# Softmax denominators of two non-local blocks: from matmuls with ones on TensorE to 32x32 transposes on VectorE

## The chip, the cores and the metric

The kernel runs on one core of a Trainium2 chip. The metric is the device time of one execution in microseconds (us). All data are float32. Engines are named as in the profile: PE is TensorE (PEld its weight loads), DVE is VectorE, ACT is ScalarE, SP is SyncE, which here only issues transfers (DMAs).

## The reference, cut to what matters

The input x has 4 images of 128 channels and 96 x 96 pixels. Two non-local blocks with weights of their own follow each other; each is

```python
g_x = maxpool2(conv1x1(x, g_w, g_b)).reshape(b, CI, -1).transpose(0, 2, 1)
theta_x = conv1x1(x, theta_w, theta_b).reshape(b, CI, -1).transpose(0, 2, 1)
phi_x = maxpool2(conv1x1(x, phi_w, phi_b)).reshape(b, CI, -1)
f = jnp.einsum('bqc,bck->bqk', theta_x, phi_x)
attn = jax.nn.softmax(f, axis=-1)
y = jnp.einsum('bqk,bkc->bqc', attn, g_x)
...
W_y = conv1x1(y, W_w, W_b)
...
return W_y + x
```

with CI = 64 inner channels, 9216 queries (pixels) and 2304 keys (pooled pixels) for each image, and a batch normalisation of W_y that is folded into the weights. Each query's softmax has one denominator: the sum of 2304 exponentials. This change is about these sums, their inverses, and how the inverses get to where they are multiplied.

## The kernel before

**Tiles.** An image and a layer make a block; there are 8, in the order of ORDER. A block's 9216 queries are taken in 9 *pairs* of 1024, two halves of 512 queries each; 72 pairs in all. Keys come in 18 tiles of 128. For a key tile, `scores` puts exp(theta . phi - 35) of 128 keys by 1024 queries into an `exp` tile (four matmuls of 64x64 by 512 columns, one ACT operation), `add_up` adds the tile into the pair's `sum` (128 x 1024) on DVE, and `values` accumulates values times exponentials in PSUM (`av`, four matmuls). Every matmul of the program is two instructions in the trace. A constant shift of 35 takes the place of the row maximum; whether it was enough is checked at the end from notes of all denominators and inverses.

**Steps.** The loop over `t` makes a step out of two key tiles of one pair. A pair has 9 steps, and a *cycle* has 18, s = 0 to 17: the even pair of the cycle in steps 0 to 8, the odd one in 9 to 17. In step t PE does the scores of step t and then the values of step t - 1. The order on PE, DVE, ACT and SP is the order in which the program's text issues the instructions[...]. Into the steps other work is put by hand: `first` goes between the two scores of a step, `second` after them, ahead of the values; `take` between the step's two adds on DVE; the rest behind the values.

**A pair's end.** After its last values, ACT copies `av` to `halves` (128 x 1024), and DVE adds its two halves into y (128 x 512) in `add_halves`. The column sums of `sum` over 128 partitions are the denominators. Half of each pair's partitions lies in the wrong place for that, so `move` sends 64 partitions of `sum` (256 KB) by a DMA on SP's queue to the tile `folded`, and `fold` adds the other 64 on DVE (L422). In step 2 of the next cycle (SUMS), `denominators` multiplies `folded` with a matrix of ones (L494): this sums over partitions and puts each result on 64 partitions at once. ACT takes the result out of PSUM (L413) and notes its sum; DVE inverts it in four pieces of 128 columns (L409), one a step; ACT notes the sum of the inverses (L426); DVE multiplies y with them (`normalise`, L433).

**The projection.** `multiply` (L439) projects y by W into two banks of PSUM, and `add` (L448) adds the shift and x on DVE and, for the second layer, stores 1024 columns of x to memory. The even pair is normalised in step 6 and projected in step 8, the odd one in 10 and 12 (PROJECT).

**Shared banks.** Two banks of PSUM (`misc`) serve in turn the denominators, the thetas (step 5), the chunks of the next block's keys (three steps of a cycle: 13, 15 and 17, in three cycles of each block; each goes on into the step after it, where DVE pools its result), and the projections.

Of the kernel before, what the change touches and what calls it, by code (L numbers as in the profile page):

```python
# [32 lines left out]
PT = 2 * QT  # L33
NP = HW // PT
KB = 2
NB = NKT // KB
FIRST = 6
KEYS = (15, 17, 31)
THETAS, SUMS, PROJECT = 5, 2, (8, 12)
EXPS = 7  # L40
WARM = (5, 3)
CYCLE = 2 * NB
ORDER = ((0, 0), (1, 0), (0, 1), (2, 0), (1, 1), (3, 0), (2, 1), (3, 1))
# [3 lines left out]

@with_exitstack
def shifted_blocks(ctx: ExitStack, tc: tile.TileContext, x: bass.AP, layers, out: bass.AP, flag):

# [19 lines left out]
    nc = tc.nc  # L70

    const = ctx.enter_context(tc.tile_pool(name="const", bufs=1))
# [3 lines left out]
    work = ctx.enter_context(tc.tile_pool(name="work", bufs=2))  # L76
# [13 lines left out]
    nc.vector.memset(nshift, -SHIFT)  # L90
    ones = const.tile([P, CI], F32, name="ones")
    nc.vector.memset(ones, 1.0)
    dens = const.tile([P, len(ORDER) * NP + 1], F32, name="dens")
    recs = const.tile([P, len(ORDER) * NP + 1], F32, name="recs")
    for t in (dens, recs):
        nc.vector.memset(t, 0.0)

    def load_x(b, n=6):
        xt = xp.tile([C, HW], F32, tag="x", name=f"x_{b}")
# [90 lines left out]
    def two_banks(name):  # L190
        return [ps_misc.tile([P, QT], F32, tag="misc", name=f"{name}_{i}") for i in range(2)]
# [108 lines left out]
    class Pair:  # L300
# [74 lines left out]
        def last_denominators(self):  # L375

            n = QT // 2
            self.rc, notes = self.sum[:, :QT], []
            for i in range(2):
                den = ps_sc.tile([P, PT], F32, tag="sc", name=f"den_last_ps_{i}")[:, :n]  # L380
                for part in (self.sum, self.es[NKT - 1]):
                    for h in range(2):
                        nc.tensor.matmul(
                            den[ts(h, CI), :], lhsT=ones,
                            rhs=part[:, h * QT + i * n : h * QT + (i + 1) * n],
                            start=part is self.sum, stop=part is not self.sum,
                        )
                notes.append(den)
            for i in (0, 1):
                for k in range(n // P):  # L390
                    nc.vector.reciprocal(
                        self.rc[:, ts(i * n // P + k, P)], notes[i][:, ts(k, P)]
                    )
                if i == 0:
                    self.sum_up(notes[1], dens, 1)
            self.sum_up(notes[0], dens, 0)
            for i in range(2):
                self.sum_up(self.rc[:, ts(i, n)], recs, i)

        def sum_up(self, src, to, i):  # L400

            n = self.number + i
            nc.scalar.activation(
                self.th[:, : src.shape[1]], src, AF.Identity, accum_out=to[:, n : n + 1]
            )

        def inverses(self, src, pieces=range(QT // P)):
            for i in pieces:
                nc.vector.reciprocal(self.rc[:, ts(i, P)], src[:, ts(i, P)])  # L409

        def take_denominators(self, ps, to):
            n, self.rc = self.number, to
            nc.scalar.activation(to, ps, AF.Identity, accum_out=dens[:, n : n + 1])  # L413

        def move(self, folded):

            i = self.number % 2
            nc.sync.dma_start(out=folded[ts(i, CI), :], in_=self.sum[ts(1 - i, CI), :])

        def fold(self, folded):  # L420
            here = ts(self.number % 2, CI)
            nc.vector.tensor_add(folded[here, :], folded[here, :], self.sum[here, :])  # L422

        def note(self, to):
            n = self.number
            nc.scalar.activation(to, self.rc, AF.Identity, accum_out=recs[:, n : n + 1])  # L426

        def add_halves(self):
            self.y = self.halves[:, :QT]
# [25 lines left out]
        def finish(self, check, result):  # L455
# [20 lines left out]
            for i in range(2):  # L476
# [6 lines left out]
                    nc.sync.dma_start(out=self.blk.store[:, first : first + n], in_=dst)  # L483
                if i == 0:
                    result(good)

    def denominators(both, folded):

        pss = two_banks(f"den_ps_{both[0].name}")

        def make():
            for h in range(2):
                for i in range(len(both)):
                    nc.tensor.matmul(  # L494
                        pss[i][ts(h, CI), :], lhsT=ones[ts(i, CI), :],
                        rhs=folded[ts(i, CI), ts(h, QT)], start=True, stop=True,
                    )

        def take():
            for pair, ps in zip(both, pss):  # L500
                pair.take_denominators(ps, pair.halves[:, QT:])

        return make, take

    def thetas(both):
        pss = two_banks(f"theta_ps_{both[0].name}")
# [41 lines left out]
    pairs = [Pair(blk, p, n * NP + p) for n, blk in enumerate(blocks) for p in range(NP)]  # L548
    total = len(pairs) * NB
# [43 lines left out]
    for n in range(1, len(blocks)):  # L593
        cycle = (n - 1) * NP * NB // CYCLE * CYCLE
        for j in range(NB):
            t = cycle + KEYS[j % len(KEYS)] + j // len(KEYS) * CYCLE
# [2 lines left out]
                centres[t + 2] = blocks[n]  # L599
            if j % len(KEYS) == len(KEYS) - 1:  # L600
                spreads[t + 2] = (blocks[n], j // len(KEYS))
    loads = {4 * NB + 4: 2, 31 * NB + 4: 3}
    late = len(pairs) - 2

    ends = {
        total - 3: (NKT - 8,), total - 2: (NKT - 7,), total - 1: (NKT - 6, NKT - 5),
        total: range(NKT - 4, NKT),
    }
    folded, gone, pending = None, [], (None, None)
    for t in range(total + 1):  # L610
        q, s = 2 * (t // CYCLE), t % CYCLE
        even, odd = pairs[q : q + 2] if t < total else (None, None)
        first, second, take = None, *pending
        pending = (None, None)
        if t in keys:
            n, i = keys[t]
            if n and i == 0:
                begin(n)
            first, *pending = blocks[n].chunks(i)
        elif t < total and s == (THETAS if q else THETAS + 1):  # L620
            if q < late:
                first, *pending = thetas(pairs[q + 1 : q + 3])
            else:
                first, take = odd.theta_alone()
        elif gone and s == SUMS:
            second, take = denominators(gone, folded)
        elif q == late and s == 11:
            second, take = denominators([even], folded)
        elif t == total - 1:
            second, take = even.multiply, even.add  # L630
        elif gone and s in PROJECT:
            pair = gone[PROJECT.index(s)]
            second, take = pair.multiply, pair.add
        if t < total:
            now, j = divmod(t, NB)
            if s == 0 and q:
                pairs[q - 1].move(folded)
                gone = pairs[q - 2 : q]
            if s == NB:
                folded = work.tile([P, PT], F32, tag="folded", name=f"folded_{q}", bufs=1)  # L640
                even.move(folded)
            if t in loads:
                xs[loads[t]] = load_x(loads[t])
        for i in range(KB):
# [3 lines left out]
                first()  # L648
        if second:
            second()  # L650
        if gone and s == 1:
            gone[1].fold(folded)
        if q == late and s == 10:
            even.fold(folded)
        for i in range(KB):
            if t < total:
                pairs[now].add_up(j * KB + i)
# [1 line left out]
                take()  # L659
        if t - 1 in keys and t < NB:  # L660
            b0.batch(keys[t - 1][1])
        if t == total - 1:
            even.note(even.rc)
        if gone and s in (PROJECT[0] - 1, PROJECT[1] - 1):
            pair = gone[s // (PROJECT[1] - 1)]
            pair.note(pair.rc)
        if t:
            before, j = divmod(t - 1, NB)
            for k in ends.get(t, range(j * KB, (j + 1) * KB)):
                pairs[before].values(k)  # L670
        if t < total:
            for i, pair in enumerate(gone):
                if s == 1:
                    pair.add_halves()
                k = s - PROJECT[i] + 5
                if k in range(QT // P):
                    pair.inverses(pair.rc, (k,))
                if k == QT // P - 1:
                    pair.normalise()
            if s == 13 and q < late:  # L680
                even.fold(folded)
            if q == late:
                if s == 10:
                    even.add_halves()
                if s - 12 in range(QT // P):
                    even.inverses(even.rc, (s - 12,))
                if s == 15:
                    even.normalise()
        if t == total - 1:
            odd.last_denominators()  # L690
        if t in centres:
# [17 lines left out]
    def check():  # L709

        ps = ps_sc.tile([P, PT], F32, tag="sc", name="good_ps")[:1, :1]
        nc.vector.tensor_reduce(good[:, 0:1], dens, AX.X, ALU.add)
        nc.vector.tensor_scalar(good[:, 1:2], good[:, 0:1], SUM_MAX, None, ALU.is_le)
        nc.vector.tensor_reduce(good[:, 0:1], recs, AX.X, ALU.add)
# [314 lines left out]
```

## Time and profile before

| | |
|---|---|
| median of 3 runs | 2527.51 us (2527.16 to 2528.47) |
| the profiled execution | 2528.21 us |
| its span, first to last instruction | 2526.1 us |
| granted TensorE clock | 0.999 |
| DMA traffic | 60.12 MB, mean 24 GB/s |
| PE instructions | 23342 |

The span is what the views of the trace cover; 2.1 us of the profiled execution lie outside it. In a line of a group, the fields are: line of the program, engine, operation, output and inputs, shapes, count, busy us and mean ns of one, and the engine's idle time just before them with what ended it. In a list of waits: who waited for whom, us in total, times, the longest. In a timeline: start, us from the first start to the last end, what, how many; where a line merges several instructions, their number is behind the x. Line numbers here and in the groups are those of the kernel before.

### The profile page before, as it was taken

The numbers are of one execution on the slowest core, as the hardware profiler recorded it, in microseconds if no ns is written. First come the engines' busy times: TensorE is split into PE (matmuls) and PEld (weight loads), VectorE is DVE, ScalarE is ACT, GpSimd is POOL, SyncE is SP. The second block draws the span as 40 slices with busy tenths as digits, with TensorE's granted clock in tenths as the row PEclk, the third lists the DMA queues.
The fourth block names the chain that finished last, engine by engine and source line by source line (L and its number), as shares of the span: only waits on it lengthen the run. The fifth ranks groups of instructions, "written<-read, shape, count | busy, mean of one in ns | idle before, by whom it ended". The sixth has DMA issues, their size and how long they took to land.

```text
span 2526.1 us, 53450 instructions
## 1 busy us (share of the span) xinstructions
PE 2514.9 (100%) x23342; PEld 908.8 (36%) x23342; DVE 2167.2 (86%) x2259; ACT 1626.7 (64%) x1795; POOL 0.7 (0%) x6
## 2 busy tenths in 40 slices
PE   9999999999999999999999999999999999999998
PEld 4333333333333333333333333333333333333333
DVE  7888888888888888888888888888888888888888
ACT  5666666666666666666666666666666666666665
POOL 0000000000000000000000000000000000000000
PEclk9999999999999999999999999999999999999999
DMA  4020000000000000020000000000000000000001
GB/s 159 5 85 9 10 10 5 10 9 10 10 18 14 26 26 26 18 80 10 10 10 18 23 17 26 26 18 9 6 10 10 24 20 14 26 26 26 26 26 40
DMA packets 16661, 60.12 MB, mean 24 GB/s; under 512 B 2650, under 2 KB 3556, under 8 KB 16420
## 3 DMA queue, kind: packets, MB, share of 16 engines
q1 hardware_dynamic: 16252, 56.57, 7.4%
q8 instruction: 184, 3.01, 0.5%
q14 instruction: 57, 0.47, 0.1%
q10 hardware_dynamic: 168, 0.07, 0.0%
HBM read 19.14 MB, written 18.87 MB: 15 GB/s over the span
## 4 chain that ended last, share of the span: by engine, by line


## 5 line engine op out<-in xcount | busy, mean ns | idle before, releaser
L349 ACT ACTIVATE exp<-sc,nshift 128x1024 f32<-128x1024 f32 x1296 | 1386.1, 1113 | 814.5 <-PE sc L343 814.4
L358 DVE TENSOR_TENSOR sum<-sum,exp 128x1024 f32<-128x1024 f32 x1151 | 1408.2, 1223 | 258.0 <-ACT exp L349 207.7
L343 PE MATMUL sc<-theta,phi 64*64 64x512 f32 x10368 | 1251.0, 589 | 0.8 <-ACT exp L349 0.8
L366 PE MATMUL av<-exp,gT 64*64 64x512 f32 x10368 | 1232.3, 589 | 0.0
L366 PEld LDWEIGHTS av<-exp,gT 64*64 64x64 f32 x10368 | 399.8, 133 | 713.0 <-issue 689.6
L343 PEld LDWEIGHTS sc<-theta,phi 64*64 64x64 f32 x10368 | 399.2, 133 | 712.9 <-issue 649.1
L409 DVE RECIPROCAL halves<-halves 128x128 f32<-128x128 f32 x284 | 268.5, 945 | 0.0
L200 PE MATMUL gphi_ps<-x,gphiT 64*64 64x512 f32 x1056 | 137.3, 589 | 0.0
L356 DVE TENSOR_TENSOR sum<-exp,exp 128x1024 f32<-128x1024 f32 x72 | 88.1, 1224 | 49.2 <-ACT exp L349 48.5
L226 DVE TENSOR_REDUCE gphi<-gphi_ps 128x128 f32<-128x512 f32 x144 | 92.6, 684 | 31.5 <-PE gphi_ps L200 24.6
L373 ACT COPY halves<-av 128x1024 f32<-128x1024 f32 x71 | 71.9, 1012 | 49.8 <-PE av L366 49.8
L448 DVE SCALAR_TENSOR_TENSOR x<-W_ps,shift,x 128x512 f32<-128x512 f32 x142 | 99.6, 743 | 0.0
L422 DVE TENSOR_TENSOR folded<-folded,sum 64x1024 f32<-64x1024 f32 x71 | 86.4, 1216 | 1.3 <-DMA folded<-sum 0.2
L439 PE MATMUL W_ps<-halves,WT 64*64 64x512 f32 x568 | 74.2, 590 | 0.0
L296 DVE STREAM_TRANSPOSE gT<-gphi 32x192 f32<-32x192 f32 x192 | 70.6, 368 | 3.5
L200 PE MATMUL theta_ps<-x,thetaT 64*64 64x512 f32 x560 | 72.8, 589 | 0.0
L200 PEld LDWEIGHTS gphi_ps<-x,gphiT 64*64 64x64 f32 x1056 | 45.0, 132 | 68.3 <-issue 61.2
L433 DVE TENSOR_TENSOR halves<-halves 128x512 f32<-128x512 f32 x71 | 49.1, 692 | 2.4
L430 DVE TENSOR_TENSOR halves<-halves 128x512 f32<-128x512 f32 x71 | 45.7, 685 | 0.0
L426 ACT ACTIVATE halves<-halves 128x512 f32<-128x512 f32 x71 | 44.6, 628 | 0.3 <-DVE halves L433 0.3
L413 ACT ACTIVATE halves<-den_ps 128x512 f32<-128x512 f32 x71 | 41.8, 602 | 1.6 <-DVE halves L430 1.5
L494 PE MATMUL den_ps<-folded,ones 64*64 64x512 f32 x284 | 37.4, 589 | 0.0
(78 smaller groups left out, 236.0 us busy)
## 6 DMA issues: line engine op xcount, KB each, us to landing
folded<-sum SPq DMA_DIRECT2D x71, 256.0 KB
out_dram<-x SPq DMA_DIRECT2D x35, 512.0 KB
x<-in_x_dram SPq DMA_DIRECT2D x18, 768.0 KB
x<-in_x_dram SPq DMA_DIRECT2D x12, 384.0 KB
out_dram<-x SPq DMA_DIRECT2D x4, 128.0 KB
gphi_nat<-in_L_conv_phi_w_dram SPq DMA_DIRECT2D x2, 32.0 KB
rows_other<-in_L_conv_g_b_dram SPq DMA_DIRECT2D x4, 0.2 KB
W_nat<-in_L_conv_W_w_dram SPq DMA_DIRECT2D x2, 32.0 KB
```

The source lines that it names most:

```text
L200: nc.tensor.matmul(out, lhsT=lhsT, rhs=rhs, start=step == 0, stop=step == 1)
L226: nc.vector.tensor_reduce(self.gphi[:, ts(k, KT)].rearrange("p (h w) -> p h w", w=w), ps.rearrange("p (h a w b) -> p h w a b", a=2, b=2, w=w),
L343: nc.tensor.matmul(ps[ts(c, CI), ts(h, QT)], lhsT=self.blk.phi[ts(h, CI), ts(2 * k + c, CI)], rhs=self.th[ts(h, CI), :], start=True, stop= ...
L349: nc.scalar.activation(e, ps, AF.Exp, bias=nshift)
L356: nc.vector.tensor_add(self.sum, self.es[0], e)
L358: nc.vector.tensor_add(self.sum, self.sum, e)
L366: nc.tensor.matmul(self.av[ts(h, CI), ts(r, QT)], lhsT=self.blk.gT[ts(r, CI), k, :], rhs=e[ts(r, CI), ts(h, QT)], start=(k == 0), stop=(k ...
L373: nc.scalar.copy(self.halves, self.av)
L409: nc.vector.reciprocal(self.rc[:, ts(i, P)], src[:, ts(i, P)])
L422: nc.vector.tensor_add(folded[here, :], folded[here, :], self.sum[here, :])
L439: nc.tensor.matmul(self.pss[h][ts(c, CI), :], lhsT=self.blk.w.W[ts(h, CI), ts(c, CI)], rhs=self.y[ts(h, CI), :], start=True, stop=True,)
L448: nc.vector.scalar_tensor_tensor(dst, self.pss[h], self.blk.w.shift, dst, op0=ALU.add, op1=ALU.add)
```

## The change

The matmuls with ones, `folded`, its moves and its adds go. In their place DVE works on the pair's `sum` itself (`turn`): each half of 512 columns is transposed in 32x32 squares within its partitions, and the 32 columns of each square are summed, so that a sum over 32 partitions stands in one column. `invert` transposes the four quarters of the result into one 32-partition tile, sums over the four, inverts all 1024 denominators as one square of 32 x 32, and notes both sums on DVE. Then four DMAs on SP's queue bring the inverses to the 64 partitions of each half: two write 16 rows of 32 values as one row of 512 on partition 0 and on partition 64 of `turned`, and two spread that row over 64 partitions of `halves`, where the columns already summed into y are free.

The schedule changes with it: `turn` in steps 10 and 11 (even pair) and 3 and 4 of the next cycle (odd), `add_halves` and `invert` in 12 and 5, `normalise` in 1 and 8 of the next cycle, the projections in 2 and 9. For the odd pair the inverses thus have steps 5 to 8 of one cycle, for the even pair steps 12 to 1. The last even pair is normalised in step 15 and projected in the last step, as before; the last pair of all keeps its matmuls with ones (`last_denominators`). The load of the third image moves two steps back.

```diff
-THETAS, SUMS, PROJECT = 5, 2, (8, 12)
+THETAS = 5
+HALVES, TURNS, INVERT, NORM, PROJECT = (12, 5), (10, 3), (12, 5), (1, 8), (2, 9)
+SQ = 32
...
-    dens = const.tile([P, len(ORDER) * NP + 1], F32, name="dens")
-    recs = const.tile([P, len(ORDER) * NP + 1], F32, name="recs")
...
+    notes = const.tile([P, len(ORDER) * NP + 1, 2], F32, name="notes")
+    nc.vector.memset(notes, 0.0)
...
-        def inverses(self, src, pieces=range(QT // P)):
-            for i in pieces:
-                nc.vector.reciprocal(self.rc[:, ts(i, P)], src[:, ts(i, P)])
-
-        def take_denominators(self, ps, to):
-            n, self.rc = self.number, to
-            nc.scalar.activation(to, ps, AF.Identity, accum_out=dens[:, n : n + 1])
-
-        def move(self, folded):
-
-            i = self.number % 2
-            nc.sync.dma_start(out=folded[ts(i, CI), :], in_=self.sum[ts(1 - i, CI), :])
-
-        def fold(self, folded):
-            here = ts(self.number % 2, CI)
-            nc.vector.tensor_add(folded[here, :], folded[here, :], self.sum[here, :])
-
-        def note(self, to):
-            n = self.number
-            nc.scalar.activation(to, self.rc, AF.Identity, accum_out=recs[:, n : n + 1])
+        def turn(self, h):
+
+            if h == 0:
+                self.turned = work.tile(
+                    [P, QT], F32, tag="turned", name=f"turned_{self.name}", bufs=1
+                )
+                self.parts = work.tile([P, SQ], F32, tag="parts", name=f"parts_{self.name}")
+            nc.vector.transpose(self.turned, self.sum[:, ts(h, QT)])
+            nc.vector.tensor_reduce(
+                self.parts[:, ts(h, QT // SQ)],
+                self.turned.rearrange("p (b k) -> p b k", k=SQ), AX.X, ALU.add,
+            )
+
+        def invert(self):
+
+            four = work.tile([SQ, P // SQ, SQ], F32, tag="four", name=f"four_{self.name}")
+            both = work.tile([SQ, 2, SQ], F32, tag="both", name=f"both_{self.name}")
+            for k in range(P // SQ):
+                nc.vector.transpose(four[:, k, :], self.parts[ts(k, SQ), :])
+            nc.vector.tensor_reduce(
+                both[:, 0, :], four.rearrange("p k q -> p q k"), AX.X, ALU.add
+            )
+            nc.vector.reciprocal(both[:, 1, :], both[:, 0, :])
+            nc.vector.tensor_reduce(notes[:SQ, self.number, :], both, AX.X, ALU.add)
+            self.rc = self.halves[:, QT:]
+            n = QT // SQ
+            for h in range(2):
+                row = self.turned[h * CI : h * CI + 1, :]
+                nc.sync.dma_start(
+                    out=row.rearrange("o (b k) -> o b k", k=SQ), in_=both[ts(h, n), 1, :]
+                )
+            for h in range(2):
+                row = self.turned[h * CI : h * CI + 1, :]
+                nc.sync.dma_start(
+                    out=self.rc[ts(h, CI), :],
+                    in_=row.unsqueeze(1).to_broadcast([1, CI, QT]),
+                )
...
-    def denominators(both, folded):
-
-        pss = two_banks(f"den_ps_{both[0].name}")
-
-        def make():
-            for h in range(2):
-                for i in range(len(both)):
-                    nc.tensor.matmul(
-                        pss[i][ts(h, CI), :], lhsT=ones[ts(i, CI), :],
-                        rhs=folded[ts(i, CI), ts(h, QT)], start=True, stop=True,
-                    )
...
-    loads = {4 * NB + 4: 2, 31 * NB + 4: 3}
+    loads = {4 * NB + 6: 2, 31 * NB + 4: 3}
...
-        elif gone and s == SUMS:
-            second, take = denominators(gone, folded)
-        elif q == late and s == 11:
-            second, take = denominators([even], folded)
...
-            for i, pair in enumerate(gone):
-                if s == 1:
-                    pair.add_halves()
-                k = s - PROJECT[i] + 5
-                if k in range(QT // P):
-                    pair.inverses(pair.rc, (k,))
-                if k == QT // P - 1:
-                    pair.normalise()
+            for i, pair in enumerate((even, gone[1] if gone else None)):
+                if pair is None:
+                    continue
+                if s in (TURNS[i], TURNS[i] + 1):
+                    pair.turn(s - TURNS[i])
+                if s == HALVES[i]:
+                    pair.add_halves()
+                if s == INVERT[i]:
+                    pair.invert()
+            for i, pair in enumerate(gone):
+                if s == NORM[i]:
+                    pair.normalise()
...
```

More of the change, by code (lines that the diff above doesn't have):

```diff
@@ L92, in shifted_blocks @@
     nc.vector.memset(ones, 1.0)
-    dens = const.tile([P, len(ORDER) * NP + 1], F32, name="dens")
-    recs = const.tile([P, len(ORDER) * NP + 1], F32, name="recs")
-    for t in (dens, recs):
-        nc.vector.memset(t, 0.0)
+    notes = const.tile([P, len(ORDER) * NP + 1, 2], F32, name="notes")
+    nc.vector.memset(notes, 0.0)
     def load_x(b, n=6):
@@ L377, in last_denominators @@
             n = QT // 2
-            self.rc, notes = self.sum[:, :QT], []
+            self.rc, dens = self.sum[:, :QT], []
             for i in range(2):
@@ L387, in last_denominators @@
                         )
-                notes.append(den)
+                dens.append(den)
             for i in (0, 1):
@@ L391, in last_denominators @@
                     nc.vector.reciprocal(
-                        self.rc[:, ts(i * n // P + k, P)], notes[i][:, ts(k, P)]
+                        self.rc[:, ts(i * n // P + k, P)], dens[i][:, ts(k, P)]
                     )
                 if i == 0:
-                    self.sum_up(notes[1], dens, 1)
-            self.sum_up(notes[0], dens, 0)
+                    self.sum_up(dens[1], 0, 1)
+            self.sum_up(dens[0], 0, 0)
             for i in range(2):
-                self.sum_up(self.rc[:, ts(i, n)], recs, i)
@@ L400, in sum_up @@
-        def sum_up(self, src, to, i):
+                self.sum_up(self.rc[:, ts(i, n)], 1, i)
+        def sum_up(self, src, what, i):
             n = self.number + i
             nc.scalar.activation(
-                self.th[:, : src.shape[1]], src, AF.Identity, accum_out=to[:, n : n + 1]
+                self.th[:, : src.shape[1]], src, AF.Identity, accum_out=notes[:, n, what : what + 1]
             )
-        def inverses(self, src, pieces=range(QT // P)):
-            for i in pieces:
-                nc.vector.reciprocal(self.rc[:, ts(i, P)], src[:, ts(i, P)])
@@ L485, in finish @@
                     result(good)
-    def denominators(both, folded):
-        pss = two_banks(f"den_ps_{both[0].name}")
-        def make():
-            for h in range(2):
-                for i in range(len(both)):
-                    nc.tensor.matmul(
-                        pss[i][ts(h, CI), :], lhsT=ones[ts(i, CI), :],
-                        rhs=folded[ts(i, CI), ts(h, QT)], start=True, stop=True,
-                    )
[L499 to L503, printed above, removed]
     def thetas(both):
@@ L608, in shifted_blocks @@
     }
-    folded, gone, pending = None, [], (None, None)
+    gone, pending = [], (None, None)
     for t in range(total + 1):
@@ L636, in shifted_blocks @@
             if s == 0 and q:
-                pairs[q - 1].move(folded)
                 gone = pairs[q - 2 : q]
-            if s == NB:
-                folded = work.tile([P, PT], F32, tag="folded", name=f"folded_{q}", bufs=1)
-                even.move(folded)
             if t in loads:
@@ L650, in shifted_blocks @@
             second()
[L651 to L654, printed above, removed]
         for i in range(KB):
@@ L661, in shifted_blocks @@
             b0.batch(keys[t - 1][1])
[L662 to L666, printed above, removed]
         if t:
@@ L671, in shifted_blocks @@
         if t < total:
-            for i, pair in enumerate(gone):
-                if s == 1:
-                    pair.add_halves()
-                k = s - PROJECT[i] + 5
-                if k in range(QT // P):
-                    pair.inverses(pair.rc, (k,))
-                if k == QT // P - 1:
-                    pair.normalise()
[L680 to L688, printed above, removed]
+            for i, pair in enumerate((even, gone[1] if gone else None)):
[7 more added lines that the diff above has]
+                    pair.invert()
+            for i, pair in enumerate(gone):
+                if s == NORM[i]:
+                    pair.normalise()
+            if q == late and s == 15:
+                even.normalise()
         if t == total - 1:
@@ L711, in check @@
         ps = ps_sc.tile([P, PT], F32, tag="sc", name="good_ps")[:1, :1]
-        nc.vector.tensor_reduce(good[:, 0:1], dens, AX.X, ALU.add)
+        nc.vector.tensor_reduce(good[:, 0:1], notes[:, :, 0], AX.X, ALU.add)
         nc.vector.tensor_scalar(good[:, 1:2], good[:, 0:1], SUM_MAX, None, ALU.is_le)
-        nc.vector.tensor_reduce(good[:, 0:1], recs, AX.X, ALU.add)
+        nc.vector.tensor_reduce(good[:, 0:1], notes[:, :, 1], AX.X, ALU.add)
         nc.vector.scalar_tensor_tensor(
```

## The prediction

> **What bounds the kernel now.** I read the page first, then the list of waits, then the timeline of a step with nothing extra in it, then the one place where TensorE does wait for VectorE.
>
> The page's busy times, and the groups that the change touches (busy us, mean ns of one, idle before):
>
> ```profile
> PE 2514.9 (100%) x23342; PEld 908.8 (36%) x23342; DVE 2167.2 (86%) x2259; ACT 1626.7 (64%) x1795; POOL 0.7 (0%) x6
> ...
> L409 DVE RECIPROCAL halves<-halves 128x128 f32<-128x128 f32 x284 | 268.5, 945 | 0.0
> ...
> L422 DVE TENSOR_TENSOR folded<-folded,sum 64x1024 f32<-64x1024 f32 x71 | 86.4, 1216 | 1.3 <-DMA folded<-sum 0.2
> ...
> L296 DVE STREAM_TRANSPOSE gT<-gphi 32x192 f32<-32x192 f32 x192 | 70.6, 368 | 3.5
> ...
> L494 PE MATMUL den_ps<-folded,ones 64*64 64x512 f32 x284 | 37.4, 589 | 0.0
> ```
>
> A busy PE alone proves little, so the list of waits comes next:
>
> ```profile
> ACT exp L349 <- PE sc L343: 814.4, 672, 2.5
> ...
> PE sc L343 <- ACT exp L349: 0.8, 1, 0.8
> ```
>
> ScalarE waits for TensorE 672 times; TensorE waits for ScalarE once. (The chain of waits is empty for this run, so this stands in for it.) Now one step without extras, in the timeline (start, us):
>
> ```profile
> 1267.38 1.90 PE L343 MATMUL sc<-theta,phi 64*64 64x512 f32 x16
> ...
> 1268.48 2.12 ACT L349 ACTIVATE exp<-sc,nshift 128x1024 f32<-128x1024 f32 x2 [1.31 <-PE sc L343]
> ...
> 1269.10 1.90 PE L366 MATMUL av<-exp,gT 64*64 64x512 f32 x16
> ...
> 1269.63 2.56 DVE L358 TENSOR_TENSOR sum<-sum,exp 128x1024 f32<-128x1024 f32 x2 [0.88 <-ACT exp L349]
> ...
> 1270.81 1.90 PE L343 MATMUL sc<-theta,phi 64*64 64x512 f32 x16
> ```
>
> Two things are to be seen. TensorE runs like a clock: 16 instructions every 1.717 us, 0.1073 us each, so a step is 3.43 us, and 4.29 us where a group of 8 (0.86) is added. And VectorE's two adds of a step begin 2.25 us after its scores and end at 4.81, that is 1.38 us into the next step. Any matmul that TensorE doesn't issue is time won; any wait put in front of it is time lost in full.
>
> The wait, at the end of the run, where one pair is normalised just ahead of its projection (separate timelines of DVE and PE):
>
> ```profile
> 2506.10 0.69 DVE L433 TENSOR_TENSOR halves<-halves 128x512 f32<-128x512 f32 x1
> ```
> ```profile
> 2505.00 1.99 PE L343 MATMUL sc<-theta,phi 64*64 64x512 f32 x16
> 2506.84 1.09 PE L439 MATMUL W_ps<-halves,WT 64*64 64x512 f32 x8
> 2507.75 0.61 PE L366 MATMUL av<-exp,gT 64*64 64x512 f32 x4
> ```
>
> The projection was due at 2505.00 + 1.72 = 2506.72 and began at 2506.84, 0.05 after the product ended (2506.79). What follows it began 0.91 later instead of 0.86. So a late product costs its lateness plus 0.05 to be seen plus 0.05 for weights not loaded ahead.
>
> Last, what a transfer's partitions do to its rate (columns: stretch, us, engines' busy time, clock, DMA share, GB/s). The move of 64 partitions was issued at 1275.65; the last row is a store of 128 partitions:
>
> ```profile
> 1275.60:1276.70 1.10, 1.10 (x16) 0.39 (x12) 0.02 (x1) 1.10 (x2) 0.00 (x0) 1.00 0.00 0
> 1276.80:1278.00 1.20, 1.20 (x16) 0.46 (x12) 0.49 (x1) 0.75 (x2) 0.00 (x0) 1.00 0.95 198
> 1278.30:1279.30 1.00, 1.00 (x12) 0.30 (x8) 0.97 (x2) 1.00 (x2) 0.00 (x0) 1.00 0.00 0
> 2495.10:2496.50 1.40, 1.40 (x17) 0.48 (x12) 1.40 (x3) 1.20 (x2) 0.00 (x0) 1.00 0.93 375
> ```
>
> Data flow 1.1 us after the issue, with the engines equally busy, and at half the rate: 198 against 375 GB/s.
>
> [...]
>
> **The change part by part.**
>
> *Removed from TensorE:* 284 instructions at 0.1073 us = 30.5 us. Sure, because PE never waits now.
>
> *ScalarE:* per pair, take (602 + 215 ns) and note (628 + 194) go. It waits 814 us for PE already; worth nothing.
>
> *VectorE, per pair.* Removed: 4 x 0.945 + 1.216 = 5.0 us. Added: two transposes of 128x512 at 0.70 (estimate: 368 ns for 192 elements gives some 0.17 fixed, plus 512 at 1.05 ns, the slope between the 512- and 1024-element adds, 685 and 1223 ns); two reductions of 512 at 0.68 (L226); four small transposes at 0.2; a reduction of 128 (0.28), a reciprocal of 32 columns (0.35, a quarter of L409's slope), a reduction of 64 (0.22); and 0.1 for each of five results read at once. Some 5.0 us. So its total stays; what matters is where it lies. Bounds 4.3 to 6.
>
> *Backlog.* A step has 3.43 - 2.47 = 0.96 us of room. Steps 10, 11 and 12 take 1.5, 1.5 and 2.7 extra, so the adds of step 13 start some 2.5 us late. Seven exp buffers cover over two steps, so scores don't stop. But in cycles with a chunk at 13 and at 15 (14 of them) the pools of step 14 end about 5.5 us after its scores, and the chunk of step 15 needs their banks at 4.29 + 0.86 = 5.15: 0.3 us, 4 us in all (0 to 12).
>
> *The projections.* They move from two steps behind the product to one (product at the end of steps 1 and 8, projection in 2 and 9, after the two scores). Due: 3.43 + 1.72 = 5.15 us after step 8's scores. The product starts when the second add is nearly out (4.73), takes 0.69, ends 5.42: 0.27 late, plus 0.05 and 0.05 = 0.37. In step 1 the exps run 0.06 later, behind the copy of the other pair's halves: 0.43. The last even pair keeps its distance. 35 x (0.37 + 0.43) = 28 us. If the product's two waits for transfers cost 0.1 each time, 35; if the adds run 0.1 earlier, 21.
>
> *The transfers.* One move of 256 KB becomes four: two of 16 runs of 128 bytes into a row, and two of that row to 64 partitions. All are on SP's queue, and the second kind waits there for the first. From the reciprocal's end R: two issues (0.46 each, as the move); data 1.1 after an issue; some 0.3 more until it is seen (the tail's move: issued 2480.32, last packets out about 2482.9, fold at 2483.27); second hop issued at R + 1.75, its data from R + 2.85. For the even pair 7 steps pass before the product: hidden. For the odd pair R is about 7.8 us after step 5's scores (adds start 3.2 in step 5 by the backlog of 3 and 4, end 5.7; halves 6.3; the chain to the reciprocal 1.5). The product could start at 4.29 + 4.29 + 3.43 + 4.73 = 16.74. So 8.9 us are there. Data of the second hop: 64 x 2 KB from one partition, twice. Lower bound: only the written side counts, 128 KB at 198 GB/s = 0.65 each, all in at R + 4.6. [...] 8.3 us, in at R + 11.4, 2.45 late. 35 x 2.45 = 86 us. Behind the waiting product stand the next step's adds on VectorE, and the projection on TensorE waits for it; both go late by the same. x loads move from step 4 to 6, behind the odd pair's transfers, so they don't stand in front.
>
> *Sum.* The profiled execution took 2528.2 us around a span of 2526.1; the median of the runs is 2527.5, 0.7 below. -30.5 + 28 + 4 + 86 = +87.5, and 2527.5 + 87.5 = 2615.
>
> **The rivals.**
>
> A: the row's transfers land in time. For it: writes may be all that the 198 GB/s shows; 8.9 us is twice a hop. Against: a source of one partition is the extreme of what halved the rate. Then -30.5 + 28 + 4 = +1.5: 2529, from 2518 to 2540.
>
> B, the other side: the short lead doesn't bite, and the matmuls saved stay saved. Its place is the product at the end of steps 1 and 8; its price 30.5 us gained less 70 stalls; with transfers in time it is faster by over 5 us where a stall is under (30.5 - 5) / 70 = 0.36 us on average. My 0.40 is only 0.04 above, and a second add that starts 0.1 earlier is enough. Against: the tail shows the wait for the same two instructions. Time 2507, from 2497 to 2522.
>
> C: [...] 18.9 us of data, 12 to 13 late, 35 x 12.5 = 440: 2970. Or small transposes and waits lengthen R by 1 to 2 us: 2650 to 2690.
>
> That the denominators aren't moved at all is excluded: the matmuls with ones are gone but for the last pair's.
>
> **How the numbers follow.** Forecast (late transfers) 0.47, its own range 2545 to 2665; A 0.30; B 0.15; C 0.08. A measurement here tells 0.2%, 5 us, from no change. A gives slower 0.13, same 0.15, faster 0.02. So slower 0.47 + 0.08 + 0.13 = 0.68, same 0.15, faster 0.17. The range 2508 to 2670 leaves out the lower half of B (0.08) and C's far end with the forecast's top (0.1).
>
> **What would show it.** PE instructions down by 284. In the waits, W_ps behind halves on some 70 occasions, about 0.4 each for even pairs and 2 to 3 us for odd ones; if even and odd are alike, the transfers were in time. VectorE's product in step 8 idle for a DMA. [...] If W_ps never waits, the forecast and A are both wrong.

## The result, and the profile after

The changed kernel takes 2641.6 us (median of 4 runs, 2636.2 to 2646.5) beside 2527.8 (4 runs) of the kernel before on the same chip: a ratio of 1.045, 95% interval 1.043 to 1.047. It is 114 us slower. The forecast was 2615 with a range of 2508 to 2670. The profiled execution took 2642.9 us around a span of 2641.0, so its span is 114.9 us longer than that of before.

The page after: the engines' busy times, the busiest DMA queue (packets, MB, share of 16 engines) and the groups that the change touches (busy us, mean ns of one, then idle time ahead and what ended it). Line numbers from here on are those of the kernel that a view belongs to:

```profile
PE 2543.3 (96%) x23058; PEld 980.0 (37%) x23058; DVE 2128.9 (81%) x2684; ACT 1542.8 (58%) x1511; POOL 0.7 (0%) x6
...
q1 hardware_dynamic: 26476, 56.88, 19.1%
...
L461 PE MATMUL W_ps<-halves,WT 64*64 64x512 f32 x568 | 85.3, 672 | 85.1 <-DVE halves L455 85.1
...
L455 DVE TENSOR_TENSOR halves<-halves 128x512 f32<-128x512 f32 x71 | 48.9, 689 | 71.0 <-DMA halves<-turned 71.0
L420 DVE TENSOR_REDUCE parts<-turned 128x16 f32<-128x512 f32 x142 | 97.4, 686 | 4.9
L419 DVE STREAM_TRANSPOSE turned<-sum 128x512 f32<-128x512 f32 x142 | 100.0, 704 | 0.0
```

Three things are to be seen. TensorE has its 284 instructions fewer (23342 before), and is nevertheless busy for 96% instead of 100%. VectorE is 38 us less busy (2167.2 before), so it isn't the amount of its work that costs. The rows of lines 461 and 455 are a chain: the product idles 71.0 us for a DMA, the projections behind it 85.1 us for the product. The list of waits has the same chain (us in total, times, longest):

```profile
PEld W_ps L461 <- DVE halves L455: 147.7, 71, 4.6
...
PE W_ps L461 <- DVE halves L455: 85.1, 71, 3.7
...
DVE halves L455 <- DMA halves<-turned: 71.0, 36, 3.0
```

Before, the projection (W_ps) waited for the product once, the 0.7 us of a weight load near the end; now it waits in all 71 pairs, while the product waits for a DMA in 36: 35 odd ones and the last even one. One odd pair in the timeline of after (start us, length us, engine, line, idle before):

```profile
856.38 1.90 PE L348 MATMUL sc<-theta,phi 64*64 64x512 f32 x16
...
857.49 2.12 ACT L354 ACTIVATE exp<-sc,nshift 128x1024 f32<-128x1024 f32 x2 [1.31 <-PE sc L348]
...
859.59 0.69 DVE L455 TENSOR_TENSOR halves<-halves 128x512 f32<-128x512 f32 x1 [1.84 <-DMA halves<-turned]
...
860.34 1.56 PE L461 MATMUL W_ps<-halves,WT 64*64 64x512 f32 x8 [2.06 <-DVE halves L455]
...
861.65 3.19 PE L371 MATMUL av<-exp,gT 64*64 64x512 f32 x16
...
864.66 1.90 PE L348 MATMUL sc<-theta,phi 64*64 64x512 f32 x16
```

VectorE is idle for 1.84 us until the transfer is seen, multiplies, and 0.06 us later the projection starts, TensorE having idled for 2.06 us by this view, whose matmul ends are modelled. The values behind it don't pass it: in all 71 pairs they start after the last of the projection's 8 instructions. An even pair, 29 us earlier, in the same view:

```profile
830.70 0.69 DVE L455 TENSOR_TENSOR halves<-halves 128x512 f32<-128x512 f32 x1
...
831.44 1.09 PE L461 MATMUL W_ps<-halves,WT 64*64 64x512 f32 x8 [0.18 <-DVE halves L455]
```

No DMA is waited for here; the product runs as soon as VectorE is free, and the projection starts 0.05 after its end. That is the short lead alone.

The odd stall has a second cost that the forecast didn't have: the 16 value instructions at 861.65 take 3.19 us instead of 1.90. The windows of after show why (stretch, us, busy time of PE, PEld, DVE, ACT, POOL, TensorE's granted clock, DMA share, GB/s):

```profile
856.40:858.10 1.70, 1.70 (x20) 0.44 (x12) 1.25 (x2) 0.61 (x1) 0.00 (x0) 1.00 0.57 25
858.30:860.30 2.00, 0.00 (x0) 0.00 (x0) 0.69 (x1) 1.31 (x2) 0.00 (x0) 1.00 0.09 9
861.00:864.20 3.20, 3.20 (x20) 0.87 (x16) 2.27 (x3) 0.00 (x0) 0.00 (x0) 0.50 0.03 5
864.70:868.10 3.40, 3.40 (x37) 1.19 (x33) 1.13 (x1) 3.04 (x3) 0.00 (x0) 1.00 0.22 90
```

After two idle microseconds the clock is granted at 0.50 for a while, then at 1.00 again: 20 instructions in 3.20 us, where the last row has 37 in 3.40. In the trace's record of the clock this happens after 21 of the first 34 odd stalls, each time for 3.41 us. The 35th, near the end of the kernel, is longer (3.9 us) and has 6.83 us at half clock.

Where the 114.9 us come from, by the distances of TensorE's instructions in groups of four (0.429 us in the steady state of both kernels; every group that took longer is counted once):

- 71 groups less: -30.5
- 35 even projections, late by 0.44 on average: +15.5
- 35 odd ones, late by 2.36 on average (median 2.30): +82.7
- the second half of each projection: +5.7, of which some 3.5 are 0.05 each for weights not loaded ahead (in the trace they are loaded as the projection starts, those of the values in the even pair above 0.43 us ahead; the values follow 0.91 us after the projection's start instead of 0.86), and 2.2 the few that fell under half clock
- the other groups at half clock: +36.0
- start and end of the kernel: +4.7, of which 2.3 are the last even pair's projection, whose product also waits for its transfers (3.0 us)

The sum is +114.1.

### The profile page after: what moved, and what is told of

Its sections match the earlier page's. It is cut to its first block, busy times and chain, and to the rows that moved or that the text cites. A ratio compares the mean times of both kernels' runs of the same rounds, so it can differ in the third digit from the quotient of the medians.

```text
span 2641.0 us, 53355 instructions
## 1 busy us (share of the span) xinstructions
PE 2543.3 (96%) x23058; PEld 980.0 (37%) x23058; DVE 2128.9 (81%) x2684; ACT 1542.8 (58%) x1511; POOL 0.7 (0%) x6
## 4 chain that ended last, share of the span: by engine, by line
## 5 line engine op out<-in xcount | busy, mean ns | idle before, releaser
L371 PE MATMUL av<-exp,gT 64*64 64x512 f32 x10368 | 1274.3, 602 | 0.0
L348 PE MATMUL sc<-theta,phi 64*64 64x512 f32 x10368 | 1268.3, 590 | 0.8 <-ACT exp L354 0.8
L371 PEld LDWEIGHTS av<-exp,gT 64*64 64x64 f32 x10368 | 439.2, 135 | 699.8 <-issue 639.3
L348 PEld LDWEIGHTS sc<-theta,phi 64*64 64x64 f32 x10368 | 438.3, 134 | 684.8 <-issue 613.5
L378 ACT COPY halves<-av 128x1024 f32<-128x1024 f32 x71 | 71.9, 1012 | 201.9 <-PE av L371 201.9
L461 PE MATMUL W_ps<-halves,WT 64*64 64x512 f32 x568 | 85.3, 672 | 85.1 <-DVE halves L455 85.1
L361 DVE TENSOR_TENSOR sum<-exp,exp 128x1024 f32<-128x1024 f32 x72 | 87.8, 1220 | 23.4 <-ACT exp L354 22.7
L420 DVE TENSOR_REDUCE parts<-turned 128x16 f32<-128x512 f32 x142 | 97.4, 686 | 4.9
L419 DVE STREAM_TRANSPOSE turned<-sum 128x512 f32<-128x512 f32 x142 | 100.0, 704 | 0.0
L461 PEld LDWEIGHTS W_ps<-halves,WT 64*64 64x64 f32 x568 | 15.0, 134 | 147.7 <-DVE halves L455 147.7
L430 DVE STREAM_TRANSPOSE four<-parts 32x32 f32<-32x32 f32 x284 | 56.4, 198 | 2.9
L205 PEld LDWEIGHTS theta_ps<-x,thetaT 64*64 64x64 f32 x560 | 21.7, 133 | 38.4 <-issue 29.0
```

The costliest lines, as they stand in the source:

```text
L205: nc.tensor.matmul(out, lhsT=lhsT, rhs=rhs, start=step == 0, stop=step == 1)
L348: nc.tensor.matmul(ps[ts(c, CI), ts(h, QT)], lhsT=self.blk.phi[ts(h, CI), ts(2 * k + c, CI)], rhs=self.th[ts(h, CI), :], start=True, stop= ...
L361: nc.vector.tensor_add(self.sum, self.es[0], e)
L371: nc.tensor.matmul(self.av[ts(h, CI), ts(r, QT)], lhsT=self.blk.gT[ts(r, CI), k, :], rhs=e[ts(r, CI), ts(h, QT)], start=(k == 0), stop=(k ...
L378: nc.scalar.copy(self.halves, self.av)
L419: nc.vector.transpose(self.turned, self.sum[:, ts(h, QT)])
```

## The experiments

Eight kernels were run. Each modifies the changed kernel; the kernel before takes 2527.6 to 2527.9 us in each comparison, and ratios are to it.

**e1: the second pair of transfers reads 64 partitions instead of one.**

```diff
-                    in_=row.unsqueeze(1).to_broadcast([1, CI, QT]),
+                    in_=self.turned[ts(h, CI), :],
```

> The second pair of transfers reads 64 different partitions of the square's buffer instead of one row read 64 times; bytes, packets and issues stay as they are. The denominators that normalise the averages are therefore not the reference's; everything else is computed as in the changed kernel. Theory (the row's partition limits the rate, so the data of the second pair arrive late): the odd projection's wait falls from about 2.3 to about 0.4 us, as the even one's, the windows of half clock go, and the time is 2527.8 - 30.5 + 35 x 2 x 0.44 + 6 + 3 = about 2537, between 2529 and 2542. Rival (the chain ahead of the transfers, or the fixed time of four transfers, makes them late, whatever partition they read): the odd wait stays at 2 us or more and the time stays between 2625 and 2645.

Measured: 2529.6 us, ratio 1.001 (1.000 to 1.002), clock 0.999. The windows of e1 over the data of an odd pair, then its list of waits:

```profile
959.10:960.40 1.30, 1.30 (x16) 0.46 (x12) 1.12 (x1) 1.16 (x2) 0.00 (x0) 1.00 0.86 186
```
```profile
PEld W_ps L461 <- DVE halves L455: 73.4, 70, 1.6
...
PE W_ps L461 <- DVE halves L455: 7.2, 36, 0.7
```

The same 256 KB flow at 186 GB/s, and the product waits for no DMA any more. In the packets of the trace the last byte is in 4.3 us after the end of the reciprocal (R below; median of the odd pairs), against 10.7 in the changed kernel. So 112 us of the 114 hang on the one row that is read 64 times; the chain ahead of it and the fixed time of the four transfers are not it, and the side written to is the same in both. What is left are the 0.37 us (even) and 0.31 us (odd) of the short lead, median of 35 each; with the 0.05 of each second half they eat the 30 us that the missing matmuls gain.

**e2: the odd product and projection one step later.**

```diff
-HALVES, TURNS, INVERT, NORM, PROJECT = (12, 5), (10, 3), (12, 5), (1, 8), (2, 9)
+HALVES, TURNS, INVERT, NORM, PROJECT = (12, 5), (10, 3), (12, 5), (1, 9), (2, 10)
```

> The odd pair's product and projection go one step later (9 and 10), with the same distance of one step between them; transfers as in the changed kernel. Theory (lateness of the transfers is one term, the short lead another): 3.4 us more for the transfers hide them, the wait for a DMA goes, but the odd projection still waits about 0.4 us for the product, like the even one: about 2537, between 2529 and 2542, PE's clock back at 0.999. Rival (the odd wait comes from VectorE's work at that place and not from the transfers): it moves with the product, and the time stays above 2600. Second rival (with the transfers in time there is no wait left): 2500.

Measured: 2524.6 us, ratio 0.999 (0.998 to 0.999). The transfers are in time, as expected, but neither the 2537 nor the 2500 came out: the even projection still waits (0.37), the odd one doesn't, though its lead is one step too. The timeline of e2 in step 9 has the reason:

```profile
961.68 1.90 PE L348 MATMUL sc<-theta,phi 64*64 64x512 f32 x16
...
964.94 1.23 DVE L361 TENSOR_TENSOR sum<-exp,exp 128x1024 f32<-128x1024 f32 x1 [1.89 <-ACT exp L354]
...
966.08 0.69 DVE L455 TENSOR_TENSOR halves<-halves 128x512 f32<-128x512 f32 x1
...
966.83 1.08 PE L461 MATMUL W_ps<-halves,WT 64*64 64x512 f32 x8
```

In the first step of a pair the sum is begun with one add of two tiles (L361), not two adds. The product starts 4.40 us after the step's scores (961.68), and is out at 5.09. The projection is due at 5.15. Where two adds stand ahead of it, as in steps 1 and 8, the second is out later and the product with it: e1 has the even projection late by 0.37 us and the odd one by 0.31. So the stall isn't the price of a lead of one step as such, but of the second add that stands ahead of the product.

**e3: two steps between product and projection for both pairs: the even product a step earlier, the odd product where it was, the odd projection a step later.**

```diff
-HALVES, TURNS, INVERT, NORM, PROJECT = (12, 5), (10, 3), (12, 5), (1, 8), (2, 9)
+HALVES, TURNS, INVERT, NORM, PROJECT = (12, 5), (10, 3), (12, 5), (0, 8), (2, 10)
```

> Products at the ends of steps 0 and 8, projections in 2 and 10: two steps between them, as before the change. Theory (both terms are put right; only the saved matmuls are left): -30.5 plus 2 to 5 us at head and tail, 2499 to 2503, a ratio to the kernel before of about 0.989. The product of step 8 still waits about 2 us for its transfers, on VectorE alone, and the exps' buffers hide that. Rival (VectorE, held up 2 us in step 8, makes ScalarE and then TensorE late): waits of scores on adds or exps show up in step 9 or 10, and the time is 2515 or more. Second rival (the lead of one step costs nothing, as the sum of e2 would show): same as e2.

Measured: 2509.7 us, ratio 0.993 (0.992 to 0.994): faster than before, but 7 us above the upper end of what was expected. The projections no longer wait; what does, in 14 cycles, is the chunk of step 15 (timeline of e3, at the end of a cycle):

```profile
428.03 1.28 DVE L231 TENSOR_REDUCE gphi<-gphi_ps 128x128 f32<-128x512 f32 x2
...
428.76 0.19 PEld L205 LDWEIGHTS gphi_ps<-x,gphiT 64*64 64x64 f32 x2 [0.50 <-DVE gphi L231]
```

The weights of the chunk are loaded only when VectorE has pooled the first of two banks of the chunk before. That holds TensorE up by 0.27 us, and some microseconds later the first values of a pair wait 0.16 for ScalarE's copy of the halves (L378); over 14 cycles some 4 us and 2 us. The first is the small term of the forecast that the changed kernel doesn't show. Neither the theory nor a rival had the measured time.

**e4: one transfer for both rows.**

```diff
-            for h in range(2):
-                row = self.turned[h * CI : h * CI + 1, :]
-                nc.sync.dma_start(
-                    out=self.rc[ts(h, CI), :],
-                    in_=row.unsqueeze(1).to_broadcast([1, CI, QT]),
-                )
+            rows = self.turned.rearrange("(h c) k -> h c k", h=2)[:, 0, :]
+            nc.sync.dma_start(out=self.rc, in_=rows.unsqueeze(1).to_broadcast([2, CI, QT]))
```

> The second hop is one transfer of both rows (source two partitions, each read 64 times) instead of two transfers of one row each; the same 128 packets of 2 KB. Theory (each row's partition has its own limited rate, and two transfers on one queue go mostly one after the other): with both rows read side by side the data take about half as long, in at R + 7 to 8 instead of R + 10.7, the odd wait falls to the even one's 0.4, and the time is 2529 to 2542. Rival (the rate is limited where both rows share it, or the order of packets in the queue stays the same): in at R + 9 to 11, the odd wait above 1 us, the time 2590 to 2640.

Measured: 2542.2 us, ratio 1.006 (1.004 to 1.007), the upper end of the theory; last data at R + 8.7, later than the 7 to 8 of the theory and sooner than the 9 to 11 of the rival, the odd wait 0.45 us (median of 35; the largest 2.2). The windows over the data, of e4 and then of the changed kernel (presumably from row 0 at first, then from row 64 as well):

```profile
965.00:969.00 4.00, 4.00 (x44) 1.42 (x40) 3.02 (x3) 2.44 (x3) 0.00 (x0) 1.00 0.13 51
```
```profile
998.20:1001.20 3.00, 3.00 (x36) 1.07 (x32) 2.45 (x2) 1.69 (x3) 0.00 (x0) 1.00 0.95 30
1001.20:1005.60 4.40, 3.58 (x36) 1.04 (x28) 2.45 (x2) 3.09 (x4) 0.00 (x0) 1.00 0.59 36
```

A DMA share of 0.13 is what 2 engines of 16 make. Two engines, presumably one for each row, moved 51 GB/s, where all 16 together (share 0.95), presumably most of them at the first row, moved 30. The changed kernel's high DMA share was mostly waiting: a packet of 2 KB took 0.084 us in e4 and 0.8 in the changed kernel. But in e4 the packets follow one another without a gap in two streams, 0.084 us each, so two engines may have a limit of their own, and e4 alone doesn't say whether engines or rows set the 51 GB/s. e8 reads both rows with more engines.

**e8: the second hop in eight transfers, the rows in turn.**

```diff
-            for h in range(2):
-                row = self.turned[h * CI : h * CI + 1, :]
-                nc.sync.dma_start(
-                    out=self.rc[ts(h, CI), :],
-                    in_=row.unsqueeze(1).to_broadcast([1, CI, QT]),
-                )
+            for g in range(4):
+                for h in range(2):
+                    row = self.turned[h * CI : h * CI + 1, :]
+                    nc.sync.dma_start(
+                        out=self.rc[h * CI + g * 16 : h * CI + g * 16 + 16, :],
+                        in_=row.unsqueeze(1).to_broadcast([1, 16, QT]),
+                    )
```

> The changed kernel with the second hop in eight transfers instead of two: 16 partitions each, one from row 0, the next from row 64, and so on in turn, each over all the DMA engines. e4 read both rows side by side, but with 2 of the 16 engines alone. Theory (what limits is what one row's partition gives; two rows read at the same time give twice that): the issues, some 0.6 us each, pace it at 32 KB in 0.6 us = 54 GB/s; last data at R + 8 to 9 instead of R + 10.7, the odd wait 0.4 to 0.8, no half-clock windows, 2532 to 2555. Rival (transfers on one queue go one after the other, each at one row's rate, however they are cut): [...] last data at R + 10.5 or later, odd wait 2 us or more, 2630 or more.

Measured: 2536.7 us, ratio 1.004 (1.003 to 1.005), last data at R + 8.6, odd wait 0.40 (median). The windows over the data:

```profile
1030.50:1034.50 4.00, 4.00 (x44) 1.50 (x40) 3.02 (x3) 2.69 (x3) 0.00 (x0) 1.00 0.84 55
```

Again nearly twice the rate of the first row alone (55 beside 30 GB/s), now with a DMA share of 0.84. Since the issues themselves come at 32 KB in 0.63 us (52 GB/s; two issues of the changed kernel are 0.61 apart), the two rows may have more to give, and what set e4's 51 GB/s stays open. What e8 shows is that reading the two rows in turn gave 55 GB/s, so its transfers weren't held to one row's rate by being on one queue.

**e7: more bytes from the first row.**

```diff
+            more = work.tile([CI // 2, 448], F32, tag="more", name=f"more_{self.name}", bufs=1)
+            nc.sync.dma_start(
+                out=more, in_=self.turned[:1, :448].unsqueeze(1).to_broadcast([1, CI // 2, 448])
+            )
```

> The changed kernel with one more transfer per pair ahead of the second pair: 448 elements of the first row to 32 partitions of a tile that nobody reads (57 KB). Theory (what a row's partition gives[...] sets when the data are in[...]): the odd wait grows by 1.7 to 2.1 us to 4.0 to 4.4, that is 60 to 74 us, and nearly all of the 35 odd stalls bring a half-clock window instead of 21, about 24 us more: 2722 to 2742. Rival (half clock follows something else, about as often as before): 2700 to 2716. Second rival (the engines, not the row, limit: 57 KB more at the 190 GB/s of e1): 2641 + 35 x 0.3 = 2652.

Measured: 2766.6 us, ratio 1.094 (1.092 to 1.096). The list of waits of e7, then its span with the mean granted clock:

```profile
PE W_ps L465 <- DVE halves L459: 165.1, 71, 6.0
DVE halves L459 <- DMA halves<-turned: 150.7, 36, 5.2
```
```profile
core 0: 2763.3 us, clock 0.963
```

57 KB more put the last data from R + 10.7 to R + 12.8: 26 GB/s, near the 30 of the changed kernel's first window. The odd wait is 4.5 us instead of 2.3 (+78 us in all), a little beyond what the theory said (60 to 74 us); the time is 25 us above its range, mostly because the cost of the clock was taken too low. The trace's record has a half-clock stretch after all of the first 34 odd stalls, where the changed kernel had 21. That was about as expected, an estimate from the changed kernel's 21 of 34; but 21 of the 34 stretches last 6.83 us in place of 3.41. Half clock costs about 81 us here, 36 in the changed kernel: the price grows faster than the stall.

**e5 and e6: two ways to a faster kernel.** e5 is e3 with the even pair's chain a step earlier; e6 takes the odd pair's chain two steps earlier instead and leaves the odd projection in 9.

```diff
-HALVES, TURNS, INVERT, NORM, PROJECT = (12, 5), (10, 3), (12, 5), (1, 8), (2, 9)
+HALVES, TURNS, INVERT, NORM, PROJECT = (11, 5), (9, 3), (11, 5), (0, 8), (2, 10)
```

> As e3 (products 0 and 8, projections 2 and 10), with the even pair's chain one step earlier: turned in 9 and 10, halves and inverse in 11. e3 took 2509.7, some 6 us over what the saved matmuls alone leave; in its trace the chunk of step 15 waits 0.3 us for the pools of step 14 in 14 cycles, and what follows some 0.2 more: the backlog of VectorE from steps 10 to 13. Theory: the backlog is worked off a step earlier and these waits go: 2502 to 2505. Rival (the odd projection's adds in step 10 and the turn now meet in the same step, and the backlog only moves): 2508 to 2511.

```diff
-HALVES, TURNS, INVERT, NORM, PROJECT = (12, 5), (10, 3), (12, 5), (1, 8), (2, 9)
+HALVES, TURNS, INVERT, NORM, PROJECT = (12, 3), (10, 1), (12, 3), (0, 7), (2, 9)
```

> The other way to two steps of lead: the odd pair's chain two steps earlier (turned in 1 and 2, halves and inverse in 3), products in 0 and 7, projections in 2 and 9 as in the changed kernel. Theory (the projection stays in 9, so its adds are off VectorE before the even pair is turned in 10, as in the changed kernel, where the chunk of step 15 didn't wait): no wait of projections, none of chunks, 2501 to 2505, ratio about 0.990. Rival (the even product, the odd turn and two adds together in steps 0 to 3 make scores late there): 2508 or more, with waits of scores or of the odd chunk of step 15 in the trace.

Measured: e5 2501.6 us, ratio 0.990 (0.988 to 0.991), 0.4 below the theory's range; e6 2505.1, ratio 0.991 (0.990 to 0.993), at the upper end of its theory. e5 is 26 us faster than before, 140 faster than the change as made, the best of all. The page of e5, then its list of waits:

```profile
PE 2486.1 (99%) x23058; PEld 1219.3 (49%) x23058; DVE 2122.1 (85%) x2684; ACT 1540.6 (62%) x1511; POOL 0.7 (0%) x6
```
```profile
DVE halves L455 <- DMA halves<-turned: 69.1, 36, 3.0
...
PEld W_ps L461 <- DVE halves L455: 2.4, 2, 1.2
```

The first line of the waits is the lesson of the case. VectorE still waits 69.1 us for the same late transfers, as it waited 71.0 in the changed kernel. But the projection is two steps off, so TensorE doesn't hear of it. Of the 30.5 us that the matmuls gave, 26 arrive; the rest is at the start and the end of the kernel. In e5 the chunk of step 15 no longer holds TensorE up in 14 cycles (0.2 us in all). In e6 the waits of the chunk are there, but small: twelve of 0.06 us and twelve of 0.12 behind them, 2.2 us.

## Why the prediction was right, and where it wasn't

*Removed matmuls, -30.5.* Right: the change's instruction count fell by 284, and e5 gets 26 us of it once nothing else stands in the way.

*Short lead, +28.* Right in size: e1, where of the waits in the cycle only this is left, has 15.4 us for even and 11.5 for odd projections, and 3.5 for the second half of each, whose 0.05 the forecast's 0.40 also holds: 30.5 in place of 28. Its time, 2529.6, is that of rival A (2529), with the transfers in time; that the two agree so closely is partly luck, since A's sum had 4 us for a chunk that costs nothing there, and 2.5 too few for the short lead. Rival B, the faster side, is excluded there: the average stall is 0.43 us (0.38 without the second half), over the 0.36 below which B would have been faster. The reason was right too, though e2 sharpens it: it is the second add in front of the product.

*Row transfers, +86.* The mechanism was right, and e1, e4, e7 and e8 show it. The size was a little high: the odd projection is late by 2.36 - 0.31 = 2.05 us instead of 2.45, so +72. The last even pair, for which nothing had been counted, is late by 2.3 as well. The margin was read well (8.9 us; without a wait the product starts at R + 9.06 in e1), and so was the start of the data (R + 2.85; 2.9). The 8.3 us for the data were the author's estimate, as were rival C's 18.9; nothing in the trace of before shows the rate of a single row. The changed kernel moved the 256 KB in 7.75 us, 34 GB/s. What sets the rate of a row, 26 GB/s in e7 and 30 in the changed kernel's first window, no run shows.

*Chunk of step 15, +4.* Not in the changed kernel: 0. In e3 the same wait costs 4 us, and 2 more follow from it or beside it. It had been worked out for a TensorE that doesn't wait in the cycle; in the changed kernel and in e1 projections stall in steps 2 and 9, and VectorE gains on it meanwhile. That this is the reason is argued from e6, where those stalls are gone and the wait is back at 0.06 us; no run shows it alone.

*What was missing: the clock, +36 and the 2.2 within projections.* The forecast priced a stall by its length alone. Here a stall that leaves TensorE idle for 2.2 to 2.5 us is followed by 3.41 us at half clock in 21 of 34 cases. This (+38), the start and end (+4.7) and the short lead's 2 us too few are more than the whole distance between 2615 and 2641.6; the transfers' 14 us and the chunk's 4 us too many went against it. So it is in part luck that the sum came within 27 us. The range, 2508 to 2670, was wide enough to hold rival A and half of B too, so that the time lies in it says less than the list of waits does.

*VectorE.* Some 5.0 us per pair were forecast for the added work, 0.1 of it for each result read at once: before, the product (L433) starts 0.03 us after the end of the reciprocal that it reads, while a reciprocal starts 0.08 before the end of an add that it doesn't read. Transposes, reductions and reciprocal take 4.5 us, and 0.2 are idle between them. That its total would hardly change (it fell by 38 us in all) and doesn't decide was right.

## What to carry to other kernels

Work taken off the bottleneck engine is only gained if nothing is put in front of it in exchange. Give each result that it consumes the slack of its slowest supplier: e5 has the same late transfers as the changed kernel and is 5% faster, for five numbers in a line. To spread a row over partitions, count the partitions that are read as well as bytes and engines: one partition read 64 times gave 26 to 30 GB/s, two gave 51 to 55, and 64 gave 186. And a stall of the bottleneck engine is to be priced with what it does to the clock afterwards: here 38 us on top of 83.

## What was not expected of the hardware

Stalls of little over 2 us were followed by half clock. The first 34 odd stalls idle TensorE for 2.2 to 2.5 us, counted from the end of the last four instructions at their pace of 0.43 us, and 21 of them are followed by 3.41 us at half clock (6.83 for 21 of 34 in e7, where the odd wait is 4.5 us). The length doesn't tell the 21 from the others: they idle for 2.22 to 2.51 us, the other 13 for 2.24 to 2.41. In the changed kernel's record of the clock, the starts of all its 24 half-clock stretches lie whole multiples of 3.413 us apart (for instance 71.68 or 68.27 us from the end of one to the start of the next, 21 and 20 times 3.413). Laid over this spacing, each of the 21 stalls covers at least 0.61 of one interval; of the 13 others, eleven cover at most 0.59 and two cover 0.64. So the share covered doesn't explain every case, and why these two differ is open. Waits of 0.4 us in e1, e4 and e8 didn't do it, nor did the three longest in the cycles of e4 and e8, 2.15 to 2.23 us late: the granted clock of the profiled executions was 0.999 in e1 and e8 and 1.000 in e4, and 0.999 before the change.

A transfer whose source is two rows kept only as many DMA engines busy as 2 of 16 (share 0.13), and its data were still in 2 us earlier (R + 8.7) than those of two transfers with a share of up to 0.95 (R + 10.7).
